# A reordered prologue in a ternary feed-forward kernel on one core: loads of W1, counting of masks, placing of gathered rows, PSUM banks

## The chip, the cores and the metric

The kernel runs on one core of a Trainium2 chip. The metric is the device time of one execution in microseconds (us); a lower one is better. Three runs of the kernel before gave a median of 972.73 us (972.67 to 972.78).

The core has four engines that compute. In the profile they are PE (TensorE: PE its matmuls, PEld the loading of their stationary operands), DVE (VectorE), ACT (ScalarE) and POOL (GpSimd). SP (SyncE) issues the transfers between HBM and the on-chip memory (SBUF), GpSimd the indirect gathers. TensorE writes its results to PSUM, eight banks of 512 f32 columns for 128 partitions. Every engine works through its own instructions in order and waits on semaphores for the others.

## The reference

```python
w = weights[conditions]                          # conditions (128,), weights (200, 64, 64)
c = jnp.einsum('bct,bcd->bdt', x, w)             # x (128, 64, 512)
def ternarize(W, threshold):                     # threshold 0.05
    absW = jnp.abs(W)
    delta = threshold * jnp.max(absW)
    mask = absW > delta
    n = jnp.maximum(jnp.sum(mask), 1)
    alpha = jnp.sum(jnp.where(mask, absW, 0.0)) / n
    return alpha * jnp.sign(W) * mask
h = gelu(c @ ternarize(W1).T + b1)               # W1 (2048, 512), exact gelu
y = h @ ternarize(W2).T + b2                     # W2 (512, 2048)
scale = jnp.max(jnp.abs(y)) / 7 + 1e-8
out = x + jnp.clip(jnp.round(y / scale), -7, 7) * scale
```

What matters here is ternarizing. No sign of W1 is known before the maximum of all of W1 is, since the threshold delta depends on it. The factor alpha, the sum of the magnitudes above delta divided by their number, is not needed for the first product: the kernel multiplies by the ternary signs and applies alpha where the gelu reads the product. So layer 1 can run ahead of alpha, as far as there are PSUM banks to keep its products in.

## The kernel before, in words

The batch of 128 goes in `NB` = 16 groups `n` of 8 batch elements, that is of four pairs (`PAIRS`), and 512 rows (`BLK`) of the layers' input. The hidden 2048 columns are 16 chunks `hc` (`NH`) of 128. The weights are held in four quarters `g` (`NG`) of four chunks. For accuracy every value is split into a high part (f32r) and a low part (f16), so every product is two rounds of matmuls, `k = 0` with a widened f32r copy of the ternary weights and `k = 1` with the narrow ones.

All instructions go through the helper `InOrder` (line 36): each engine gets them in the order of the program, and every line of the profile reads L36. So instructions are told apart by their tiles. The order is written out by hand.

The prologue, up to about 84 us, treats group 0 separately:

- Lines 113 to 140 issue the loads on SyncE: the conditions, W1 (tiles `nat`), in the pieces of `PIECES` (line 121: quarters 0 and 1 whole, quarter 2 in two, quarter 3 in three), x of group 0, b1, W2, b2. The transfers take eight semaphores in turn, so from the ninth on an issue waits until the transfer eight issues earlier has landed.
- Line 281: 50 matmuls on a tile of ones (`idle`), whose result nobody reads.
- Lines 284 to 297: VectorE takes the maximum of |W1| by pieces (tile `top`); ScalarE writes the signs and, in place, the magnitudes of quarters 0 to 2 (`sign1`, `abs1`); quarter 3's come later.
- `fetch` (line 174) gathers 128 rows of the conditioned weights for one pair by an indirect transfer from GpSimd into a tile of its own, `place` (line 186) copies them, times 64, as two 64x64 blocks into the diagonal tile `diag`, with GpSimd. Group 0's four pairs are fetched and placed ahead of the threshold, group 1's later in the prologue.
- `thresholds` (line 229): the maximum over the partitions with one TensorE transpose (`tops_delta_w`), then delta.
- `mix0` (line 303) multiplies x by `diag` into the four `py` banks; `hi0`, `lo0` split the result with ScalarE and VectorE.
- `mask1` and `signed1` (lines 325, 331) write masks and ternary signs of W1 (`masks`, `terns`) on VectorE; `widen1` (line 371) widens one chunk of `terns` on GpSimd into one of four buffers (`wf`).
- `early(hc)` (line 517) is layer 1 for chunk hc of group 0: 4 matmuls with `wf`, 4 with `terns`, into one of five banks in turn, two `ph` and the first three `py`. The fourth `py` bank holds `number`.
- `count1` (line 339) counts the masks: ones are stationary, the masks move through in pieces of 256 columns, 8 matmuls for each quarter. `above1` (line 350) sums the magnitudes above delta on ScalarE. `alpha_1` (line 535) makes alpha: VectorE reduces `number`, TensorE adds the sums over the partitions (`total`), VectorE finishes.
- `early_bend(hc)` (line 528) needs alpha: ScalarE reads the bank with the gelu (into a `ring` tile) and copies the high part `h`. The low part is a subtraction, by GpSimd for chunks 0, 2, 4 and 6, by VectorE for the others.

The order in which these were put is in lines 611 to 684: two chunks of layer 1, the count of quarter 0, chunk 2, the count of the other quarters, then `alpha_1`, whose second half (`next(find, None)`, the matmul `total`) stands inside chunk 3, ahead of its last two matmuls:

```python
    early(2)
    for g in range(1, NG):
        count1(g, number, False, g == NG - 1)
    find = alpha_1()
    next(find)
    early(3, lambda: next(find, None))
    widen1(0, 5)
    early(4)
    early_bend(0)
    widen1(0, 6)
```

From chunk 5 on a loop (lines 676 to 681) goes through `early(hc)`, `widen1(0, hc + 2)`, `early_bend(hc - 4)` and `behind(hc)`. `behind` spreads VectorE's work on W2 over the chunks: the maxima (`largest2`), the last ternary signs of W1, the threshold, whose transpose `ahead(11)` puts in front of chunk 11, and W2's signs (`signed2`). Behind it layer 2 of group 0 runs (lines 698 to 723) between the mixes of group 1 (`condition`), which take the two `ps_c` banks in turn. The groups behind follow in lines 963 to 1128.

## Time and profile before

| | |
|---|---|
| median of three runs | 972.73 us |
| the profiled execution | 972.58 us |
| its span, first to last instruction | 970.8 us |
| mean granted TensorE clock | 0.998 |
| TensorE busy / VectorE / ScalarE / GpSimd | 99% / 68% / 63% / 68% |
| TensorE's first block of layer 1 starts | 20.32 us |
| layer 2 of group 0 starts | 53.89 us |
| TensorE busy from 54 to 84 us | 30.00 of 30 us |

The page gives shares of the span and a chain of work that ended last, followed back from the last instruction. The timeline lists each engine's instructions in order of time: start, duration (of several, from the first's start to the last's end), engine, source line, operation, the tile written and the tiles read, the shape, and how many were merged; behind it, in brackets, how long the engine had been idle and what ended that. Matmul ends are modelled, and overlap the next matmul's start; so where TensorE waits, it is better seen from the starts.

### The profile page before, as it was taken

To read this page: it belongs to the slowest core of one execution; us is meant where nothing else is said; L and a number is where in the kernel's file an instruction comes from. 1 tells how busy PE (TensorE), PEld (TensorE's weight loads), DVE (VectorE), ACT (ScalarE), POOL (GpSimd) and SP (SyncE) were. 2 spreads that over 40 slices of the span, in tenths; PEclk is the share of its full clock that TensorE was granted. 3 is DMA by queue.
4 is the path that set the end of the run, shared out by engine and by line. 5 is a ranking of instruction groups with operands and counts; after the bars stand their busy time and mean duration, and the time that the engine had idled before them with its cause. 6 is when DMAs were issued, how large, how long until landed. Compare 5 with 4: busy or idle time off the path is not lost.

```text
span 970.8 us, 16879 instructions
## 1 busy us (share of the span) xinstructions
PE 960.1 (99%) x5858; PEld 727.4 (75%) x5858; DVE 659.7 (68%) x1143; ACT 613.7 (63%) x1076; POOL 662.0 (68%) x1024
## 2 busy tenths in 40 slices
PE   8999999999999999999999999999999999999996
PEld 5677667778788787887887787787887878766664
DVE  7898766666676666666666666666766765467856
ACT  7994445656656566665656666566666666467773
POOL 6877867777676676767677676776767776466541
PEclk9999999999999999999999999999999999999999
DMA  9201011010111100111110111101011111339994
GB/s 358 99 23 47 14 34 49 24 69 15 35 49 34 59 24 35 49 33 48 34 60 15 35 49 33 59 25 55 28 33 51 33 57 48 109 128 371 392 408 180
DMA packets 33158, 80.05 MB, mean 82 GB/s; under 512 B 3760, under 2 KB 3760, under 8 KB 30128
## 3 DMA queue, kind: packets, MB, share of 16 engines
q1 hardware_dynamic: 31024, 76.86, 22.0%
q0 software_dynamic: 2048, 2.10, 0.7%
q8 instruction: 47, 0.77, 0.3%
q14 instruction: 39, 0.32, 0.1%
HBM read 46.44 MB, written 32.51 MB: 81 GB/s over the span
## 4 chain that ended last, share of the span: by engine, by line
PE 97%; DVE 2%; ACT 0%; POOL 0%; issue 0%; ACTq 0%; POOLq 0%
PE py L36 46%; PE xy L36 18%; PE z L36 14%; PE ph L36 11%; PE pc L36 6%; PE idle L36 1%; DVE masks L36 1%; DVE xt L36 0%; DVE y_last L36 0%; DVE terns L36 0%; ACT diag L36 0%; PE number L36 0%; ACT ph L36 0%; DVE ymax L36 0%; DVE low_last L36 0%
## 5 line engine op out<-in xcount | busy, mean ns | idle before, releaser
L36 PE MATMUL py<-wf,h 128*128 128x512 f32 x1056 | 309.7, 418 | 0.0
L36 POOL CAST wf<-w2t 128x512 fp32r<-128x512 fp8e4 x236 | 205.6, 889 | 116.3 <-PE py L36 113.0
L36 DVE SCALAR_TENSOR_TENSOR low_parts<-ring,h 128x512 f16<-128x512 f32 x224 | 188.5, 877 | 85.9 <-ACT h L36 85.7
L36 PE MATMUL py<-w2t,low_parts 128*128 128x512 fp8e4 x944 | 228.0, 379 | 0.0
L36 PEld LDWEIGHTS py<-wf,h 128*128 128x128 f32 x1056 | 192.0, 189 | 44.8
L36 POOL CAST wf<-sums 128x256 fp32r<-128x256 fp8e4 (+1 forms) x288 | 142.1, 498 | 78.3 <-PE xy L36 75.2
L36 ACT ACTIVATE ring<-ring,b1t,alpha_up 128x512 f32<-128x512 f32 x192 | 155.9, 818 | 56.2 <-DVE ring L36 52.0
L36 DVE TENSOR_TENSOR ring<-xy,ring 128x256 f32<-128x256 f32 x192 | 106.6, 555 | 113.2 <-PE xy L36 113.2
L36 ACT COPY ring<-xy 128x256 f32<-128x256 f32 x192 | 71.6, 373 | 176.2 <-PE xy L36 175.0
L36 POOL CAST wf<-w1t 128x256 fp32r<-128x256 fp8e4 (+1 forms) x240 | 140.4, 596 | 27.8 <-PE ph L36 23.4
L36 PEld LDWEIGHTS <-low_parts 128*128 128x128 f16 x944 | 92.1, 98 | 88.8 <-issue 1.7
L36 ACT ACTIVATE h<-ring 128x512 fp32r<-128x512 f32 x224 | 130.3, 627 | 1.1
L36 POOL TENSOR_SCALAR diag<-wg 64x64 f32<-64x64 f32 x128 | 68.0, 532 | 40.0 <-DMA wg<-in_L_cond_weights,rows 36.1
L36 PEld LDWEIGHTS <-w1t 128*128 128x128 fp8e4 x768 | 63.4, 98 | 32.8 <-issue 12.8
L36 PE MATMUL xy<-xb,wf 128*128 128x256 f32 x384 | 84.7, 302 | 0.0
L36 PE MATMUL xy<-xt,wf 128*128 128x256 f32 x384 | 75.4, 277 | 0.0
L36 PE MATMUL xy<-xl,sums 128*128 128x256 f16 x384 | 75.3, 278 | 0.0
L36 POOL DMA_INDIRECT wg<-in_L_cond_weights,rows x64 | 63.0, 985 | 16.5 <-issue 13.7
L36 PE MATMUL xy<-xl,w1t 128*128 128x256 f16 x384 | 74.3, 275 | 0.0
L36 PE MATMUL ph<-x,wf 128*128 128x512 f32 (+1 forms) x260 | 73.2, 403 | 0.1
L36 PE MATMUL z<-xl,sums 128*128 128x256 f16 x384 | 73.2, 273 | 0.0
L36 ACT ACTIVATE ring<-ph,b1t,alpha_up 128x512 f32<-128x512 f32 x48 | 37.3, 777 | 54.7 <-PE ph L36 52.5
(133 smaller groups left out, 1421.8 us busy)
## 6 DMA issues: line engine op xcount, KB each, us to landing
xt<-in_x SPq DMA_DIRECT2D x38, 512.0 KB, 8.3
y_dram<-y SPq DMA_DIRECT2D x15, 1024.0 KB, 4.3
out<-xt SPq DMA_DIRECT2D x30, 512.0 KB, 8.2
x_quarters<-in_x SPq DMA_DIRECT2D x52, 256.0 KB, 2.7
nat<-in_L_ffn_W SPq DMA_DIRECT2D x6, 1024.0 KB, 10.2
y_back<-y_dram SPq DMA_DIRECT2D x2, 1024.0 KB, 10.7
nat<-in_L_ffn_W SPq DMA_DIRECT2D x3, 512.0 KB, 8.9
wg<-in_L_cond_weights,rows POOLq DMA_INDIRECT x64, 2.5
```

The source lines that it names most:

```text
L36: return lambda *args, **kw: self._tc.keep_in_program_order(make(*args, **kw))
```

## The change

The changed kernel differs in the prologue; in the groups behind, `fetch` and `place` only name their tiles in another way (these hunks are left out of the diff below).

- W1's quarters 0 to 2 are all loaded in two halves. Maxima and signs go by halves too; the magnitudes by quarters as before.
- 44 idle matmuls instead of 50.
- The four gathers of a group go into one tile; the pool holds one such tile instead of four of a pair each. In the prologue the rows are placed by `place_all`: two copies, one for each half of the partitions, instead of eight. Group 1's are placed in `behind(8)`, after the bend of chunk 4.
- `count1` makes the masks stationary, 128 columns at a time, and moves one column of ones through: 16 matmuls for each quarter, into one PSUM column, in a `ps_c` bank. Its sum over the partitions then needs one more matmul (`all1`), so alpha is made in three steps.
- Layer 1 of group 0 uses six banks, all four `py` and two `ph`; the first mixes take other banks for that.
- The order: `widen1(0, 0)` and `(0, 1)` go ahead of the gathers for group 1, `(0, 5)` ahead of the second two. Chunks 2 and 3 go ahead of the counts of quarters 0 and 1; the counts of quarters 2 and 3 stand inside chunk 4, `all1` and `total` inside chunk 5. W2's maxima begin in `behind(6)`, two at a time at first; the transpose for W2's threshold stands inside chunk 11; W2's sums go two, one, one instead of one, one, two.

```diff
@@ -73,7 +73,7 @@
 
     const = ctx.enter_context(tc.tile_pool(name="const", bufs=1))
     big = ctx.enter_context(tc.tile_pool(name="big", bufs=20))
-    gather = ctx.enter_context(tc.tile_pool(name="gather", bufs=PAIRS))
+    gather = ctx.enter_context(tc.tile_pool(name="gather", bufs=1))
     half = ctx.enter_context(tc.tile_pool(name="half", bufs=8))
     quarter = ctx.enter_context(tc.tile_pool(name="quarter", bufs=4))
     ps_c = ctx.enter_context(tc.tile_pool(name="ps_c", bufs=2, space=PSUM))
@@ -118,7 +118,7 @@
 
     nat1, nat2 = [], []
 
-    PIECES = [[slice(0, GH)], [slice(0, GH)], [slice(0, 2), slice(2, GH)]]
+    PIECES = [[slice(0, 2), slice(2, GH)]] * 3
     PIECES.append([slice(0, 2), slice(2, 3), slice(3, GH)])
     W1f = W1.rearrange("p k c h -> p k (c h)")
     for g in range(NG):
@@ -174,19 +174,26 @@
     def fetch(n, j):
 
         pair = n * PAIRS + j
-        wg = gather.tile([P, D], F32, tag="wg", name=f"wg_{pair}")
+        if j == 0:
+            gathered[n] = gather.tile([P, PAIRS, D], F32, tag="wg", name=f"wg_{n}")
         pool.indirect_dma_start(
-            out=wg[:, :],
+            out=gathered[n][:, j, :],
             out_offset=None,
             in_=table,
             in_offset=bass.IndirectOffsetOnAxis(ap=rows[:, pair : pair + 1], axis=0),
         )
-        return wg
-
-    def place(j, wg):
+
+    def place(n, j):
         for h in range(2):
             out = diag[half_of(h), j, h * D : (h + 1) * D]
-            pool.tensor_scalar(out, wg[half_of(h), :], UP, None, ALU.mult)
+            pool.tensor_scalar(out, gathered[n][half_of(h), j, :], UP, None, ALU.mult)
+
+    def place_all(n):
+        for h in range(2):
+            out = diag[half_of(h), :, h * D : (h + 1) * D]
+            pool.tensor_scalar(out, gathered[n][half_of(h)], UP, None, ALU.mult)
+
+    gathered = {}
 
     def parts(n):
         return [
@@ -262,24 +269,26 @@
     def group1(tiles, g):
         return tiles[g // 2][:, g % 2, :]
 
-    def sign1(g):
-        act.activation(group1(signs, g), flat(nat1[g]), AF.Sign)
+    def sign1(g, part=slice(0, WCH)):
+        act.activation(group1(signs, g)[:, part], flat(nat1[g])[:, part], AF.Sign)
+
+    parts1 = slice(0, WCH // 2), slice(WCH // 2, WCH)
+
+    mags = nat1[: NG - 1]
 
     def abs1(g):
 
         if g == NG - 1:
             mags.append(big.tile([P, GH, T], F32, tag="big", name="mag"))
-        else:
-            mags.append(nat1[g])
         act.activation(flat(mags[g]), flat(nat1[g]), AF.Abs)
-
-    mags = []
 
 
     idle = ps_h.tile([P, T], F32, tag="ph", name="idle")
     pool.memset(above[:, :T], 1.0)
-    for _ in range(50):
+    for _ in range(44):
         pe.matmul(out=idle, lhsT=ones_b, rhs=above[:, :T], start=True, stop=True)
+    for j in range(PAIRS):
+        fetch(0, j)
     at = 0
     for g in range(NG):
         for ks in PIECES[g]:
@@ -292,16 +301,16 @@
             )
             at += 1
         if g < NG - 1:
-            sign1(g)
+            for part in parts1:
+                sign1(g, part)
             abs1(g)
-    fetched = [fetch(0, j) for j in range(PAIRS)]
-    for j in range(PAIRS):
-        place(j, fetched[j])
+    place_all(0)
     two_next = parts(0)
     pcs = []
 
     def mix0(j):
-        pc = ps_y.tile([P, NT, P], F32, tag=f"py{j}", name=f"pc_0_{j}")
+        home, tag = [(ps_c, "pc"), (ps_h, "ph"), (ps_y, "py0"), (ps_y, "py1")][j]
+        pc = home.tile([P, NT, P], F32, tag=tag, name=f"pc_0_{j}")
         mix(pair_of(x_next, j), j, pc)
         pcs.append(pc)
 
@@ -336,15 +345,15 @@
             ALU.mult,
         )
 
-    def count1(g, number, first, final):
-        n = number.shape[1]
-        for i in range(WCH // n):
+    def count1(g):
+        for i in range(WCH // P):
             pe.matmul(
                 out=number,
-                lhsT=ones_b,
-                rhs=group1(masks, g)[:, i * n : (i + 1) * n],
-                start=(first and i == 0),
-                stop=(final and i == WCH // n - 1),
+                lhsT=group1(masks, g)[:, i * P : (i + 1) * P],
+                rhs=ones_b[:, :1],
+                start=(g == 0 and i == 0),
+                stop=(g == NG - 1 and i == WCH // P - 1),
+                skip_group_check=True,
             )
 
     def above1(g):
@@ -353,7 +362,6 @@
             above, flat(mags[g]), AF.Relu, bias=minus1, accum_out=sums1[:, g : g + 1]
         )
 
-    parts1 = slice(0, WCH // 2), slice(WCH // 2, WCH)
     wf1 = [half.tile([P, 2, NT, P], F32R, tag="half", name=f"wf1_{i}") for i in range(2)]
     w1f = [wf1[i // 2][:, i % 2] for i in range(4)]
     cond = {0: two_next}
@@ -413,14 +421,13 @@
                     stop=(c == NT - 1 and k == 1),
                 )
 
-    def layer1_0(n, hc, ph, part=slice(0, BLK), between=None):
+    def layer1_0(n, hc, ph, part=slice(0, BLK), between={}):
         g, i = divmod(hc, GH)
         narrow = group1(terns, g)[:, i * T : (i + 1) * T].rearrange("p (c h) -> p c h", c=NT)
         for k in range(2):
             w = narrow if k else wide1[n, hc]
             for c in range(NT):
-                if between is not None and k == 1 and c == NT - 2:
-                    between()
+                between.get((k, c), lambda: None)()
                 pe.matmul(
                     out=ph,
                     lhsT=w[:, c, :],
@@ -514,9 +521,9 @@
     ring = [t[:, i, :] for t in rings for i in range(2)]
     ring += [quarter.tile([P, BLK], F32, tag="quarter", name=f"ring_{i}") for i in (10, 11)]
 
-    def early(hc, between=None):
-
-        slot = (hc + 1) % 5
+    def early(hc, between={}):
+
+        slot = (hc + 4) % 6
         if slot < 2:
             ph = ps_h.tile([P, BLK], F32, tag="ph", name=f"ph_0_{hc}")
         else:
@@ -535,8 +542,11 @@
     def alpha_1():
 
         count = const.tile([P, 1], F32, name="count1")
-        dve.tensor_reduce(count, number, AX.X, ALU.add)
-        dve.tensor_scalar(count, count, 1.0, None, ALU.max)
+        dve.tensor_copy(count, number)
+        yield
+        all_of = ps_c.tile([P, 1], F32, tag="pc", name="all1")
+        pe.matmul(out=all_of, lhsT=ones_f, rhs=count, start=True, stop=True)
+        dve.tensor_scalar(count, all_of, 1.0, None, ALU.max)
         dve.reciprocal(count, count)
         yield
         total = ps_c.tile([P, NG], F32, tag="pc", name="total1")
@@ -610,10 +620,10 @@
 
     mask1(0, parts1[0])
     signed1(0, parts1[0])
-    fetched += [fetch(1, j) for j in range(2)]
     widen1(0, 0)
     widen1(0, 1)
-    fetched += [fetch(1, j) for j in range(2, PAIRS)]
+    for j in range(2):
+        fetch(1, j)
     lo0(0)
     lo0(1)
     hi0(2)
@@ -629,41 +639,43 @@
     abs1(3)
     for g in range(NG):
         above1(g)
-    number = ps_y.tile([P, T // 2], F32, tag="py3", name="number")
-    count1(0, number, True, False)
+    early(2)
+    number = ps_c.tile([P, 1], F32, tag="pc", name="number")
+    count1(0)
     mask1(1)
     signed1(1)
     widen1(0, 4)
-    for j in range(PAIRS):
-        place(j, fetched[PAIRS + j])
+    early(3)
+    count1(1)
     mask1(2)
     mask1(3)
     signed1(2)
-    early(2)
-    for g in range(1, NG):
-        count1(g, number, False, g == NG - 1)
+    widen1(0, 5)
+    for j in range(2, PAIRS):
+        fetch(1, j)
+    widen1(0, 6)
+    early(4, {(1, 0): lambda: count1(2), (1, 2): lambda: count1(3)})
     find = alpha_1()
     next(find)
-    early(3, lambda: next(find, None))
-    widen1(0, 5)
-    early(4)
+    early(5, {(0, 2): lambda: next(find), (1, 2): lambda: next(find, None)})
+    widen1(0, 7)
     early_bend(0)
-    widen1(0, 6)
+    early_bend(1)
     wf2 = half.tile([P, 2, T], F32R, tag="half", name="wf2")
     w2f = [wf2[:, i, :] for i in range(2)]
     w2f += [quarter.tile([P, T], F32R, tag="quarter", name=f"wf2_{i}") for i in (2, 3)]
     find = thresholds("w2", top_2, above.bitcast(F32)[:, :P])
 
 
-    def ahead(hc):
-        if hc == 11:
-            next(find)
-
     def behind(hc):
-        if 5 <= hc < 5 + NG:
+        if hc == 6:
+            largest2(0)
+        if 6 <= hc < 6 + NG - 1:
             largest2(hc - 5)
         if hc == 7:
             sign1(3)
+        if hc == 8:
+            place_all(1)
         if hc == 9:
             signed1(3)
         if hc == 11:
@@ -676,9 +688,8 @@
         if hc in (13, 14):
             widen2(0, hc - 13)
 
-    for hc in range(5, NH):
-        ahead(hc)
-        early(hc)
+    for hc in range(6, NH):
+        early(hc, {(1, 2): lambda: next(find)} if hc == 11 else {})
         if hc + 2 < NH:
             widen1(0, hc + 2)
         early_bend(hc - 4)
@@ -718,10 +729,10 @@
         if hc in (5, 7, 9, 11):
             j = (hc - 5) // 2
             condition(1, j, pair_of(x_next, j), two_next)
-            for g in {7: [0], 9: [1], 11: [2, 3]}.get(hc, []):
+            for g in {7: [0, 1], 9: [2], 11: [3]}.get(hc, []):
                 sum2(g)
     cond[1] = two_next
-    x_next, two_next, fetched = [], [], []
+    x_next, two_next = [], []
     hf = ring[:2]
     widen1(1, 0)
     widen2(0, NH - LAG)
...
```

More of the change, by code (lines that the diff above doesn't have):

```diff
@@ L987, in eight @@
             if 2 <= hc < 2 + PAIRS:
-                fetched.append(fetch(n + 1, hc - 2))
+                fetch(n + 1, hc - 2)
             if 7 <= hc < 7 + PAIRS:
-                place(hc - 7, fetched[hc - 7 - PAIRS])
+                place(n + 1, hc - 7)
         if n == KNOWN and hc in (0, 1):
@@ L1089, in behind @@
                 if k < PAIRS:
-                    fetched.append(fetch(n + 1, k))
+                    fetch(n + 1, k)
                 if 2 <= k < 2 + PAIRS:
-                    place(k - 2, fetched[PAIRS * (n - 1) + k - 2])
+                    place(n + 1, k - 2)
                 if not leaves:
```

## Prediction

> **What bounds the kernel now.** I read the page's share of busy time, then the chain that ended last, then the first 90 us engine by engine in the timeline.
>
> ```profile
> PE 960.1 (99%) x5858; PEld 727.4 (75%) x5858; DVE 659.7 (68%) x1143; ACT 613.7 (63%) x1076; POOL 662.0 (68%) x1024
> ...
> PE 97%; DVE 2%; ACT 0%; POOL 0%; issue 0%; ACTq 0%; POOLq 0%
> ```
>
> TensorE is the bound, and from 31.6 us on the chain runs through it alone until the tail. So a change in the prologue is worth what it moves TensorE's position at the end of the prologue, no more: a later start of everything behind is passed on to the end one for one. I call `early(k)` block k. This is TensorE, out of its timeline:
>
> ```profile
> 2.96 13.62 PE L36 MATMUL idle<-junk,ones_b 128*128 128x512 bf16 x50 [2.96 <-POOL junk L36]
> 16.42 0.27 PE L36 MATMUL tops_delta_w<-ident_f,first 128*128 128x128 f32 x1
> ...
> 20.32 0.74 PE L36 MATMUL ph<-x,wf 128*128 128x256 f32 x4
> ...
> 24.07 1.04 PE L36 MATMUL number<-masks,ones_b 128*128 128x256 bf16 x8
> ...
> 26.80 1.91 PE L36 MATMUL number<-masks,ones_b 128*128 128x256 bf16 x16
> 29.07 1.03 PE L36 MATMUL number<-masks,ones_b 128*128 128x256 bf16 x8 [0.36 <-DVE masks L36]
> ...
> 31.32 0.28 PE L36 MATMUL total<-sums,ones_f 128*128 128x4 f32 x2
> ...
> 35.79 1.20 PE L36 MATMUL ph<-x,wf 128*128 128x512 f32 x4
> ```
>
> Block 0 starts at 20.32, the counting takes 0.82 us at 24.07 and 3.06 us (0.5 of it waiting) at 26.80, the total of the sums goes out at T = 31.32 after three and three quarter blocks, and block 6 starts at 35.79. Of the other engines these lines matter:
>
> ```profile
> 32.38 0.78 ACT L36 ACTIVATE ring<-ph,b1t,alpha_up 128x512 f32<-128x512 f32 x1 [1.31 <-PE ph L36]
> ...
> 37.70 1.91 ACT L36 ACTIVATE signs<-nat 128x2048 bf16<-128x2048 f32 x1
> ...
> 40.31 0.62 ACT L36 CAST h<-ring 128x512 fp32r<-128x512 f32 x1
> ```
> ```profile
> 41.01 2.32 POOL L36 TENSOR_TENSOR h<-ring,h 128x512 fp32r<-128x512 f32 x1 [1.79 <-ACT h L36]
> 43.28 1.16 POOL L36 CAST wf<-terns 128x512 fp32r<-128x512 bf16 x2
> ```
> ```profile
> 32.21 8.86 DVE L36 TENSOR_REDUCE top<-nat 128x1 f32<-128x2048 f32 x4
> 40.98 1.21 DVE L36 TENSOR_TENSOR terns<-masks,signs 128x2048 bf16<-128x2048 bf16 x1
> ```
>
> T starts everything on these three. The first gelu runs at T+1.06. ScalarE is then full: four bends, the last sign, bend 4, whose copy ends at T+9.6. GpSimd's subtraction for block 4 waits for that copy (its 1.79 us idle) and runs at T+9.69. Behind it in GpSimd's order stands the widening for block 11, ready at 43.89 where TensorE wanted it near 44.9: one microsecond to spare. VectorE's maxima of W2 also start at T+0.9.
>
> **Part by part.** *Start of block 0.* W1's last quarter keeps its three pieces. Its first piece lands at 12.90 (SyncE's next issue on that lane), the last at 14.41. VectorE now reaches it without backlog: 12.93 + 1.13 + two of 0.6, the last after 14.41, ends near 15.3, not 15.48. So the halves bring 0.15 us. Six idle matmuls of 0.216 us less free TensorE at 15.1, and the transpose goes at 15.9, not 16.42. Of x the halves land at 15.8 and 17.1 (issue plus 10.9 and 11.0 us), just in time; x is issued two lanes later but its queue holds W1 until 14.4, so I cost that at nothing (up to 0.5 us if the queue ran dry). The gathers land at 14.08; eight copies ended at 17.05, two end near 15.4. Signs in halves cost ScalarE three times some 0.17 us, but it starts them on the first half and ends 1 us earlier. Together block 0 starts at 19.8: gain 0.5.
>
> *The wait for block 2.* It now follows block 1 directly, at 19.8 + 1.84 + 1.91 = 23.5 (blocks at 20.32, 22.16, 24.07). Its widening needs VectorE's second half of terns, at 22.55 now (23.17 less 0.6), and runs beside VectorE's masks, where three casts took 4.66 us at 23.28, so 1.56 and not 0.6: ready at 24.2. Wait 0.7 (none if the cast ran at 0.6).
>
> *Counting.* 32 matmuls of 256 columns become 64 with one column, each with its own weights. The trace has no such matmul. From above, the 109 ns from start to start of the 256 columns; from below, 11 ns: where a bf16 weight load has nothing to hide it (behind block 1's f32 half) the next matmul comes after 227 instead of 216 ns. The two 4-column matmuls of the total start 29 ns apart. I take 29 + 11 = 40 ns, nearest to these rows: 2.6 us (0.7 to 7.0).
>
> The Trainium skill, "TensorE: Matmul & The Clock Gate", section "LDWEIGHTS (loading the stationary operand)", gives columns / 1.2 ns, 107 ns for 128, which would make 6.8 us and speaks against the change; its section on Fast Weight Load speeds up loads that are not FP32. The f32 rows agree with 107 (333 against 229 ns), the bf16 rows do not (11 ns), so the measurement decides; by the first rule the sum below would be 4.2 us more.
>
> *T.* In the new order the total stands at three quarters of block 5, not of block 3. Blocks 0 to 4 take 1.84, 1.91, 1.91 and twice 1.85, three quarters of 5 with the new column sum 1.6: 11.0 us. T = 19.8 + 11.0 + 0.7 + 2.6 = 34.1, against 31.32: **2.8 us later**, with ScalarE's sums long ready (31.06 less 0.6). That is not itself lost, as TensorE worked; what waits for T is.
>
> *Six banks.* Block 6 takes block 0's bank, which the first gelu gives back at T+1.84 plus 0.06. TensorE is done with block 5 at T+0.57. **Wait 1.3**: block 6 at 36.0, against 35.79. Five banks asked that of block 5, but a whole block lay between.
>
> *Placing the rows of group 1* (eight copies at 27.91 to 33.0 before, hidden, as block 6's widening was ready at 35.74 and TensorE there at 35.64) now stands behind the subtraction for block 4 and ahead of the widening for block 11. Both chains hang on T as before, so the subtraction again meets VectorE's signs and takes 2.27 to the next start. One 64x256 copy: from below a 64x64 one, 0.37, from above four, 1.46; 0.65 as a 512-wide cast at 0.6 is nearest. Widening ready at T + 9.69 + 2.27 + 1.3 + 0.61 + 0.05 = T+13.9 = 48.0. TensorE would be there at T + 1.9 + 1.92 + 4 x 1.805 = T+11.0. **Wait 2.9.** Block 11 with the transpose now inside ends at 48.0 + 2.0 = 50.0, against 46.67: 3.3 us late.
>
> *W2's threshold.* The transpose goes at block 11's three quarters, 49.5 against 44.94, so VectorE's full row of signs and low parts up to 74 us runs 4.55 us late, TensorE 3.3. The third mix of group 1 (74.08) needs a bank whose last reader ends at 73.50: slack 0.55, so 0.65 more (0 to 1.2, by how VectorE's passes fall beside GpSimd). Two W2 sums ahead of the third low part end near 88, TensorE needs it near 88.4: nothing. Later steps keep their order on GpSimd, gathers included, with the same waits: the one gather tile is refilled four steps after its last copy. Nothing.
>
> Sum: 3.3 + 0.65 = **4.0 us** on the profiled execution's 972.58 us (span 970.8), 976.6; the runs' median is 972.73, 0.15 from it, within what I can resolve. About 0.2%, 1.95 us, is what a measurement of this kernel can tell from no change.
>
> **Rivals.** *Forecast, 0.66:* 974.5 to 978.5, by counting at 20 to 60 ns (1.3 us either way) and row copies of 0.45 to 1.0 us. *Dear counting, 0.08:* if the 109 ns hold for one column too, T moves by 64 x 69 ns more: 4.4 us, 981.0. For it speaks that no matmul of the trace repeats faster for long, against it the 11 and 29 ns. *Nothing much, 0.16:* counting at 15 ns (1.6 us less), the cast of block 2 at 0.6 (0.7 less), the late bank of the third mix without effect (0.65 less): 4.0 - 2.95 = 1.05, so 973.6. It also covers that the edits reach less than they say, as the halves of W1 do.
>
> *Not slower, 0.10:* the counting is nearly free and TensorE's lead survives. At 11 ns T falls to 32.2 and block 6 to 34.1, 1.7 us ahead of 35.79. The lead is worth 1.7 us at the end, 970.9, if the widening for block 11 is ready when TensorE comes, at T+11.0; from there on each microsecond that it is late costs one. For it: GpSimd sat idle 1.79 us ahead of the subtraction, time enough for the two copies. Against it: in the changed order the copies stand behind the subtraction, and the subtraction waits for ScalarE, not for GpSimd.
>
> The range takes in the forecast and most of the two cases at its sides: 973.9 to 979.4. Of the chances, faster by over 0.2% is a part of the last case, 0.06; within 0.2% the rest of it and most of "nothing much" (up to 974.7), 0.16; slower 0.78.
>
> **What would show it.** The total near 34.1 (31.32); TensorE idle about 1.3 us ahead of block 6 and 2.9 ahead of block 11, the latter put down to GpSimd's casts; 64 `number` matmuls in some 2.6 us; the transpose for W2 near 49.5. Wrong if block 11 starts before 45.5, or if the counting takes over 4 us.

## The result, and the profile after

The changed kernel took 977.5 us (median of 6 runs, 976.93 to 979.17); the kernel before took 972.68 us beside it (6 runs, 972.49 to 972.78). The ratio is 1.0054, with a 95% interval of 1.0041 to 1.0067: slower by half a per cent. The forecast was 976.6 us, with a range of 973.9 to 979.4. The profiled execution took 977.55 us, with a span of 975.7 us and a mean granted clock of 0.997.

The page of the changed kernel, share of busy time and chain of work that ended last:

```profile
PE 958.8 (98%) x5886; PEld 726.3 (74%) x5886; DVE 658.7 (68%) x1145; ACT 614.1 (63%) x1079; POOL 653.4 (67%) x1012
...
PE 94%; DVE 1%; issue 1%; POOL 1%; DMA 1%; ACT 0%; SPq 0%; POOLq 0%; ACTq 0%
```

TensorE is busy 1.3 us less and the span is 4.9 us longer, so TensorE stands idle some 6 us more. GpSimd has come into the chain with 1%. Where that is, TensorE's timeline shows (start, duration, and in brackets the idle time ahead and what ended it):

```profile
16.29 0.33 PE L36 MATMUL tops_delta_w<-ident_f,first 128*128 128x128 f32 x1 [1.57 <-DVE first L36]
...
19.95 0.72 PE L36 MATMUL ph<-x,wf 128*128 128x256 f32 x4
...
24.65 1.19 PE L36 MATMUL ph<-x,wf 128*128 128x512 f32 x4 [0.66 <-POOL wf L36]
...
26.55 0.54 PE L36 MATMUL number<-ones_b,masks 128*128 128x1 bf16 x16
26.96 1.19 PE L36 MATMUL ph<-x,wf 128*128 128x512 f32 x4
...
33.56 0.28 PE L36 MATMUL total<-sums,ones_f 128*128 128x4 f32 x2
...
35.54 1.17 PE L36 MATMUL ph<-x,wf 128*128 128x512 f32 x4 [1.25 <-ACT ring L36]
...
48.03 1.96 PE L36 MATMUL ph<-x,wf 128*128 128x512 f32 x4 [3.22 <-POOL wf L36]
...
50.66 0.42 PE L36 MATMUL tops_delta_w<-ident_f,junk 128*128 128x128 f32 x1
...
51.37 1.39 PE L36 MATMUL ph<-x,wf 128*128 128x512 f32 x4
```

In the kernel before, the transpose for W2 stands just ahead of block 11, and block 12 follows:

```profile
44.94 0.27 PE L36 MATMUL tops_delta_w<-ident_f,junk 128*128 128x128 f32 x1
...
46.67 1.28 PE L36 MATMUL ph<-x,wf 128*128 128x512 f32 x4
```

Read the starts. Block 0 is at 19.95 (20.32 before), the total at 33.56 (31.32), block 6, after a wait for ScalarE to give back block 0's bank, at 35.54 (35.79). So up to here TensorE is ahead of the kernel before, by 0.25 us. Then it waits 3.22 us for block 11's widened weights, and block 12 starts at 51.37, against 46.67: 4.70 us late. The second `total`, in the groups' first part, is at 93.38 instead of 88.56 (4.82), and the span is 4.9 longer. So nearly everything was lost ahead of block 12.

Of the 4.70 the wait is only 3.22. The other part stands in the durations: block 11 took 3.34 us from start to start, where it took 1.73 before, each with the transpose. The windows of 4 us show why (busy time and instructions of PE, PEld, DVE, ACT and POOL, then the granted clock, DMA share and GB/s):

```profile
44.00:48.00 4.00, 0.81 (x4) 0.20 (x2) 1.53 (x3) 3.91 (x7) 3.85 (x5) 1.00 0.62 183
48.00:52.00 4.00, 3.97 (x11) 2.38 (x12) 0.78 (x4) 3.21 (x6) 3.45 (x5) 0.57 0.21 81
```

In the window behind the wait the granted clock is 0.57 in the mean. In windows of 0.1 us it is 1.00 until 48.1 and 0.50 from 48.2 to 51.6: TensorE, idle for 3.2 us, came back at its full clock, fell to half of it within 0.2 us and ran so for 3.4 us.

What it waited for, on GpSimd:

```profile
43.25 2.31 POOL L36 TENSOR_TENSOR h<-ring,h 128x512 fp32r<-128x512 f32 x1 [2.06 <-ACT h L36]
45.53 1.77 POOL L36 TENSOR_SCALAR diag<-wg 64x256 f32<-64x256 f32 x2
47.37 1.16 POOL L36 CAST wf<-terns 128x512 fp32r<-128x512 bf16 x2
```

GpSimd idles 2.06 us for ScalarE's copy `h` of block 4, subtracts, then places group 1's rows (1.77 us for two copies), and only then widens for block 11, which starts 0.05 us after the first of the two casts has ended. The copies need nothing that was not there 2 us earlier; they stand at that place because the order was written so.

### The profile page after: what moved, and what is told of

It is laid out like the page before. It is cut to its first block, busy times and chain, and to the rows that moved or that the text cites. A ratio compares the mean times of both kernels' runs of the same rounds, so it can differ in the third digit from the quotient of the medians.

```text
span 975.7 us, 16928 instructions
## 1 busy us (share of the span) xinstructions
PE 958.8 (98%) x5886; PEld 726.3 (74%) x5886; DVE 658.7 (68%) x1145; ACT 614.1 (63%) x1079; POOL 653.4 (67%) x1012
## 4 chain that ended last, share of the span: by engine, by line
PE 94%; DVE 1%; issue 1%; POOL 1%; DMA 1%; ACT 0%; SPq 0%; POOLq 0%; ACTq 0%
PE py L36 46%; PE xy L36 18%; PE z L36 13%; PE ph L36 10%; PE pc L36 6%; DMA nat<-in_L_ffn_W 1%; POOL wf L36 1%; DVE xt L36 0%; SPq L36 0%; POOL wg L36 0%; DVE y_last L36 0%; DVE top L36 0%; ACT diag L36 0%; POOL diag L36 0%; ACT ph L36 0%
## 5 line engine op out<-in xcount | busy, mean ns | idle before, releaser
L36 POOL CAST wf<-w1t 128x256 fp32r<-128x256 fp8e4 (+1 forms) x240 | 140.3, 595 | 28.0 <-PE ph L36 23.5
L36 POOL TENSOR_SCALAR diag<-wg 64x64 f32<-64x64 f32 (+1 forms) x116 | 65.5, 565 | 41.1 <-DMA wg<-in_L_cond_weights,rows 37.9
```

Source lines behind the costliest of these rows:

```text
L36: return lambda *args, **kw: self._tc.keep_in_program_order(make(*args, **kw))
```

## The experiments

The theory after the result: the 4.9 us are the late widening for block 11 (the row copies in front of it, and T, the total, 2.24 us later) and the clock that falls behind the wait. Rivals: that the copies' place is innocent; that the clock's fall is no part of it; that the later T costs by another way. All times below are medians, with the lowest and highest run; each ratio is to the kernel before, run beside it. What is called `e6` and so on is the name of a run.

**e1: place first.** The changed kernel with the row copies taken out of `behind(8)` and put ahead of `early_bend(4)`, so ahead of the subtraction, in GpSimd's idle time.

```diff
-        if hc == 8:
-            place_all(1)
...
             widen1(0, hc + 2)
+        if hc == 8:
+            place_all(1)
         early_bend(hc - 4)
```

> Changed kernel, with group 1's two row copies put ahead of the subtraction for block 4 on GpSimd instead of behind it; all else the same. Queue theory (block 11 waits because the copies, 1.83 us, stand between the subtraction and its widening, and the clock drops because that gap is over 3 us): the copies fit into GpSimd's 2.06 us of idle time ahead of the subtraction, block 11 starts near 46.15 instead of 48.03 with a gap of 1.5 us, at full clock, so 1.9 + 1.65 us less: near 974.0 us. Rival (the late total is the whole cause, the copies are innocent): block 11 still waits about 3 us and the time stays near 977.5.

Measured: 974.37 us (974.16 to 976.04), 1.0021 (1.0012 to 1.0030). TensorE's timeline:

```profile
45.75 1.21 PE L36 MATMUL ph<-x,wf 128*128 128x512 f32 x4 [1.36 <-POOL wf L36]
```

The wait is 1.36 instead of 3.22, and block 11 takes 1.85 us at full clock. 3.1 of the 4.9 us went by moving two instructions.

**e2: the wait filled.** The changed kernel with 52 matmuls of ones by ones ahead of block 11, whose result nobody reads; all else as it was.

```diff
+        if hc == 11:
+            filler = ps_c.tile([P, P], F32, tag="pc", name="filler")
+            for _ in range(52):
+                pe.matmul(out=filler, lhsT=ones_b, rhs=ones_b, start=True, stop=True)
         early(hc, {(1, 2): lambda: next(find)} if hc == 11 else {})
```

> Changed kernel, with 52 matmuls of 128 columns on ones, result unread, put into TensorE's gap ahead of block 11 (some 2.9 us of work in a gap of 3.2). The wait for GpSimd stays. Clock theory (the idle gap halves the granted clock for the 3.3 us behind it): block 11 still starts near 48.03 but runs at full clock, 8 matmuls in 1.95 us with the transpose and not 3.34, so 1.4 us less: near 976.1, with a smaller spread of the runs. Rival (block 11 is slow for another reason, its operands or GpSimd's traffic): still 3.3 us for block 11 and about 977.5.

Measured: 976.12 us (976.08 to 976.29), 1.0036 (1.0022 to 1.0050).

```profile
44.50 3.07 PE L36 MATMUL filler<-ones_b 128*128 128x128 bf16 x52
47.90 1.20 PE L36 MATMUL ph<-x,wf 128*128 128x512 f32 x4 [0.33 <-POOL wf L36]
```

Block 11 starts where it did (47.90, against 48.03), with useless work ahead of it instead of a pause, and 1.4 us are gone. So that part of the loss is the clock's and not the wait's. The five runs lie within 0.2 us, the six of the changed kernel over 2.2 us. A part of that spread may come from this place too, but not all: e1 and e3, where block 11 runs at full clock, also have runs 1.2 us and more above their medians (one of 11, two of nine).

**e9: before, with the copies late.** The other direction: the kernel before, with only its eight row copies of group 1 moved into `behind(8)`, behind the subtraction for block 4.

```diff
-    for j in range(PAIRS):
-        place(j, fetched[PAIRS + j])
     mask1(2)
...
+        if hc == 8:
+            for j in range(PAIRS):
+                place(j, fetched[PAIRS + j])
```

> Kernel before the change, with only the eight row copies of group 1 moved behind the subtraction for block 4 on GpSimd, where the change has its two. Queue theory: the total stays near 31.3, but block 11 (44.96) waits for its widening behind eight copies of 0.42 us and more, until 47.4 if VectorE leaves GpSimd alone and until 49 or so if W2's signs, from 46 on, hold it: 974.9 to 978, the middle 976.5. Rival (the place of the copies is innocent, the late total did it): 972.6.

Measured: 980.60 us (979.44 to 981.26), 1.0080 (1.0066 to 1.0094); more than the theory's range. TensorE, then GpSimd, then two windows:

```profile
50.16 2.07 PE L36 MATMUL ph<-x,wf 128*128 128x512 f32 x4 [5.00 <-POOL wf L36]
```
```profile
43.24 4.23 POOL L36 TENSOR_SCALAR diag<-wg 64x64 f32<-64x64 f32 x8
47.54 3.58 POOL L36 CAST wf<-terns 128x512 fp32r<-128x512 bf16 x2
```
```profile
48.00:52.00 4.00, 1.84 (x4) 1.16 (x4) 4.00 (x4) 0.82 (x2) 4.00 (x3) 0.57 0.00 0
52.00:56.00 4.00, 4.00 (x12) 2.12 (x12) 3.96 (x2) 1.40 (x2) 4.00 (x3) 0.58 0.00 0
```

The total stands at 31.26, unmoved, and still the kernel loses 8 us. So the place of the copies is enough by itself, and the rival falls. The size was off twice: the eight copies took 4.23 us and the casts behind them 1.8 each, so the wait is 5.00 us; and the clock stayed near 0.57 for two windows.

**e3: the widening for block 11 moved too.** e1, and the widening for block 11 ahead of the subtraction as well.

```diff
-        if hc + 2 < NH:
+        if hc + 2 < NH and hc != 9:
             widen1(0, hc + 2)
+        if hc == 8:
+            place_all(1)
+            widen1(0, 11)
...
```

> Changed kernel, with group 1's row copies and also the widening for block 11 ahead of the subtraction for block 4 on GpSimd. Queue theory: no gap ahead of block 11 (44.64), the widening for block 12 is ready near 46.5 where TensorE comes near 46.6; of the waits only the one for block 0's bank (1.25 us) stays. Block 12 starts near 46.6 as before the change (46.67), so near 972.6 us. Rival (the late total is the whole cause): about 977.5, or one of the later blocks takes the wait over.

Measured: 974.32 us (973.75 to 976.11), 1.0021 (1.0011 to 1.0031): a miss by 1.7 us. Block 11 no longer waits, but later ones do, and GpSimd shows why:

```profile
48.95 1.21 PE L36 MATMUL ph<-x,wf 128*128 128x512 f32 x4 [0.71 <-POOL wf L36]
...
51.58 1.21 PE L36 MATMUL ph<-x,wf 128*128 128x512 f32 x4 [0.53 <-POOL wf L36]
```
```profile
47.29 13.48 POOL L36 CAST wf<-terns 128x512 fp32r<-128x512 bf16 x9
```

GpSimd has no idle time from 40.9 to 60.8, and its nine casts take 13.48 us, 1.5 each instead of 0.6: from here VectorE works on W2's signs beside them. What GpSimd owes is only handed on to blocks 13 and 14. That the late T starts this chain is argued here, not shown; it leads to e4.

**e4: the total earlier.** The changed kernel with the counts of quarters 2 and 3 ahead of block 4, and the sums over partitions inside block 4.

```diff
-    early(4, {(1, 0): lambda: count1(2), (1, 2): lambda: count1(3)})
+    count1(2)
+    count1(3)
     find = alpha_1()
     next(find)
-    early(5, {(0, 2): lambda: next(find), (1, 2): lambda: next(find, None)})
+    early(4, {(0, 3): lambda: next(find), (1, 2): lambda: next(find, None)})
+    early(5)
```

> Changed kernel, with the counts of quarters 2 and 3 ahead of block 4 and the sum of the count and the total inside block 4 instead of block 5. The total goes near 31.75 instead of 33.56. Queue theory: the wait for block 0's bank goes (1.25 us), block 6 starts near 34.1, but the copies still stand ahead of the widening for block 11, ready near 46.2: the gap ahead of block 11 stays at 3.0 us, block 11 is 1.85 us earlier than in the changed kernel, 975.6 us with the clock drop and 974.2 without. Rival (the late total is the whole cause): all of the loss goes, 972 or less.

Measured: 976.20 us (975.31 to 979.81), 1.0037 (1.0025 to 1.0049). The total comes 11.8 us after block 0 instead of 13.6, and the wait for block 0's bank is gone. Block 11 still waits 2.93 us, and that pause, shorter than the changed kernel's, also brought the clock to 0.50, from 50.8 to 54.3 us in windows of 0.1 us. Behind block 0 the trace has block 6 1.61 us earlier than the changed kernel and block 13 1.79, and the three lowest runs (975.31 to 975.56) meet the 975.6 expected. So the later T costs some 1.8 us, most of it ahead of block 6. The other three runs lie higher, and the profiled one, the highest, showed something new, at the threshold:

```profile
17.48 0.47 PE L36 MATMUL tops_delta_w<-ident_f,first 128*128 128x128 f32 x1 [3.14 <-DVE first L36]
17.74 6.50 PE L36 MATMUL pc<-diag,xt 128*128 128x128 f32 x32
...
50.27 1.61 PE L36 MATMUL ph<-x,wf 128*128 128x512 f32 x4 [2.93 <-POOL wf L36]
```

W1's last piece landed at 15.90 here (14.33 to 14.84 in the 13 other traces), TensorE stood 3.14 us after its 44 idle matmuls, and the first 32 matmuls of the mixes took 6.50 us instead of 3.75, with a granted clock of 0.50 from 16.7 to 23.5 us. The other two high runs of e4 (976.84 and 978.21) are put down to the same, but have no profile.

**e6: both, and one widening.** e4, the row copies ahead of the first `early_bend(0)`, and the widening for block 11 ahead of `early_bend(4)`.

```diff
     widen1(0, 7)
+    place_all(1)
     early_bend(0)
...
-        if hc + 2 < NH:
+        if hc + 2 < NH and hc != 9:
             widen1(0, hc + 2)
+        if hc == 8:
+            widen1(0, 11)
...
-        if hc == 8:
-            place_all(1)
```

> Changed kernel, with three moves on hand-written places and nothing taken out: the counts of quarters 2 and 3 ahead of block 4 with the total inside block 4; group 1's two row copies ahead of the subtraction for block 0 on GpSimd (2.56 us of idle time there); the widening for block 11 ahead of the subtraction for block 4. Theory (the loss is the queue behind late alpha, not the edits themselves): total near 31.7, no wait for block 0's bank, block 11 and block 12 without a gap, block 15 ends near 52.3 where before the change it ended at 53.9; some 0.6 us come back at the third mix of group 1, so near 971.3, below the kernel before. Rival (one-column counts, six banks or the single gather tile cost by themselves): not below 973.

Measured: 973.90 us (971.91 to 974.71), 1.0008 (0.9999 to 1.0017). The median says little here: five runs lie at 971.91 to 972.40 with a mean granted clock of 0.997 to 0.999, six at 973.90 to 974.71 with 0.996. The lower ones are near the 971.3 expected. The profile, one of them, shows no wait for GpSimd behind block 2 in the prologue, but 1.77 us of idle time ahead of the threshold, and 0.75 ahead of the third mix of group 1, for VectorE.

**e7: W1 whole again.** e6, with quarters 0 and 1 of W1 loaded and signed whole, as before.

```diff
-    PIECES = [[slice(0, 2), slice(2, GH)]] * 3
+    PIECES = [[slice(0, GH)], [slice(0, GH)], [slice(0, 2), slice(2, GH)]]
...
-            for part in parts1:
-                sign1(g, part)
+            sign1(g)
```

> The same as the run with the three moves, but W1's first two quarters loaded whole and signed whole, as before the change (the maximum of quarters 0 and 1 in one pass each). Theory (the last landing of W1, not the pieces, sets the threshold): within 0.3 us of the run with the three moves, 971.3 to 971.6. Rival (the halves pay, a microsecond at VectorE): 972.3. Rival (the halves make W1 land later): 970.9.

Measured: 972.73 us (972.27 to 973.93), 1.0001 (0.9992 to 1.0010): only one of 11 runs in the upper cluster, but the others some 0.4 us higher than e6's lower cluster. Where these 0.4 us come from is not settled. VectorE ended the maxima at 15.41 in this trace and at 15.54 in e6's; over the traces it did so at 15.41 to 15.53 with whole quarters (five) and at 15.32 to 15.54 with halves (seven, without the late landings of the changed kernel's trace, 15.77, and e4's, 16.95), so they show no gain of the halves beyond 0.1 us. Why the upper cluster is nearly gone is not shown either. The idle time ahead of the threshold was 0.95 us in this profile against 1.77 in e6's, but 0.55 of that is that the 44 idle matmuls ended later, at 15.01 against 14.46.

**e8: 50 idle matmuls.** e6 with 50 idle matmuls ahead of the threshold, as the kernel before has them.

```diff
-    for _ in range(44):
+    for _ in range(50):
```

> The same as the run with the three moves, but with 50 idle matmuls instead of 44. Theory (between the last idle matmul and the threshold TensorE waits; where W1 lands late that gap passes 2 to 3 us and the clock halves for the mixes): the transpose goes 0.4 us later, so 971.7 in the middle, but without the runs that lie 2 us and more above the others. Rival (the high runs of the changed kernel come from elsewhere): the same spread as with 44.

Measured: 972.28 us (971.90 to 972.61, 11 runs), 0.9995 (0.9986 to 1.0004). The upper cluster is gone, and the edit touches little but the idle time ahead of the threshold: the six matmuls that the change took away had covered it. That the clock fell there in the upper runs is read from e4's trace and from their mean clock (0.996); none of them was profiled. Behind block 2 one wait remains, ahead of the third mix:

```profile
73.88 1.16 PE L36 MATMUL pc<-diag,xt 128*128 128x128 f32 x8 [1.13 <-DVE x L36]
```

**e10: a third bank for the mixes.** The kernel that the expectation means is e8.

```diff
-    def condition(n, j, xp, two):
-        pc = ps_c.tile([P, NT, P], F32, tag="pc", name=f"pc_{n}_{j}")
+    def condition(n, j, xp, two, space=ps_c, tag="pc"):
+        pc = space.tile([P, NT, P], F32, tag=tag, name=f"pc_{n}_{j}")
...
-            condition(1, j, pair_of(x_next, j), two_next)
+            condition(1, j, pair_of(x_next, j), two_next, *([(ps_h, "ph")] if j == 2 else [(ps_c, "pc")])[0])
```

> The kernel of the run before last but one (row copies and one widening moved ahead of block 0 and block 4, the count's chain taken into block 4, 50 idle matmuls) with one edit: the third mix of group 1 writes to one of the banks of the blocks instead of the two banks of the mixes. In that kernel's trace TensorE stood 1.1 us ahead of the third mix, put down to VectorE's addition of an earlier mix. Theory: the wait is for the bank and all of it is on the path, so it goes and nothing takes its place: 972.28 - 1.1 = 971.2 us (971.0 to 971.5). Rival: VectorE is late there anyway, and the time comes back ahead of the tiles of group 1 behind it: 972.3 us.

Measured: 971.79 us (971.54 to 972.21, 11 runs), 0.9992 (0.9983 to 1.0001): between the two. The wait at the mix is gone, and most of it comes back ten microseconds later, on VectorE's mixed rows:

```profile
83.44 1.02 PE L36 MATMUL ph<-x,w1t 128*128 128x512 f16 x4 [0.86 <-DVE x L36]
```

**e11: a count in the wait for block 2.** e10, with the count of quarter 0 ahead of block 2.

```diff
-    early(2)
     number = ps_c.tile([P, 1], F32, tag="pc", name="number")
     count1(0)
+    early(2)
```

> The kernel of e10 with the one-column count of the first quarter put ahead of block 2 instead of behind it. TensorE waits 0.66 us ahead of block 2 for GpSimd's widening in the changed kernel, and 16 such matmuls took 0.41 us there. Theory: the count moves into the wait and 0.4 us go: 0.4 us below e10, about 970.8 us. Rival: the masks of the first quarter are not ready when block 1 ends, so the count waits itself and block 2 is as late as before: the same as e10.

Measured: 971.10 us (970.89 to 972.25, 11 runs), 0.9987 (0.9978 to 0.9996), beside 972.59 of the kernel before.

```profile
23.59 0.54 PE L36 MATMUL number<-ones_b,masks 128*128 128x1 bf16 x16
24.40 1.19 PE L36 MATMUL ph<-x,wf 128*128 128x512 f32 x4 [0.27 <-POOL wf L36]
```

The wait for block 2 fell from 0.65 to 0.27, as the theory has it; that is 0.4 of the 0.7 us. The other 0.3 is not settled: in this trace the wait for VectorE's mixed rows is 0.26 us instead of e10's 0.86, and the transpose at the threshold went 0.45 us earlier, and one trace does not tell which of this is the edit's. This version is the fastest: 1.5 us below before, with the interval just clear of 1, and 6.4 below the changed kernel (the latter across two sets of runs).

**e12: the counting alone.** The kernel before with only the one-column counting.

```diff
-        for i in range(WCH // n):
+        for i in range(WCH // P):
             pe.matmul(
                 out=number,
-                lhsT=ones_b,
-                rhs=group1(masks, g)[:, i * n : (i + 1) * n],
+                lhsT=group1(masks, g)[:, i * P : (i + 1) * P],
+                rhs=ones_b[:, :1],
...
```

The hunks left out add the sum over the partitions (`all1`) inside chunk 3 and make `number` one column wide.

> The kernel before with only the counting of the change: 64 matmuls with one column each instead of 16 with 512, and the sum over the partitions by one more matmul, all in the order of before otherwise. The changed kernel's trace gave 25 ns from start to start, 1.6 us for 64, where before's 16 took 3.4 us. Theory: before's masks of the last quarter end at 29.03 us and hold the count there, and the added sum over partitions costs a part of what is left: total 0.3 to 0.4 us earlier than 31.32, 972.3 us (971.9 to 972.6). Rival: the whole 1.8 us come off: 970.9 us. Rival: the count's extra trip through VectorE costs more than it brings: 973 us or more.

The kernel before counts with 32 matmuls of 256 columns, not with 16 of 512 as the expectation says.

Measured: 973.64 us (972.43 to 975.35, 11 runs), 1.0009 (1.0000 to 1.0018). TensorE, and a window:

```profile
26.62 0.54 PE L36 MATMUL number<-ones_b,masks 128*128 128x1 bf16 x16
27.52 0.55 PE L36 MATMUL number<-ones_b,masks 128*128 128x1 bf16 x16 [0.36 <-DVE masks L36]
29.07 0.55 PE L36 MATMUL number<-ones_b,masks 128*128 128x1 bf16 x16 [1.00 <-DVE masks L36]
29.48 1.05 PE L36 MATMUL ph<-x,wf 128*128 128x512 f32 x3
```
```profile
28.00:32.00 4.00, 3.00 (x27) 2.00 (x25) 2.57 (x5) 2.72 (x4) 3.68 (x6) 0.77 0.02 7
```

The counting is 1.7 us cheaper, and the last of it starts at 29.07 exactly as before: VectorE's masks hold it. And then the clock falls, without any long wait, to 0.50 from 30.2 to 33.6 us in windows of 0.1 us.

**e13: the counting alone, pauses filled.** e12 with 5 and 15 matmuls of ones where it waited.

```diff
+        if g > 1:
+            filler = ps_c.tile([P, P], F32, tag="pc", name=f"filler_{g}")
+            for _ in range(5 if g == 2 else 15):
+                pe.matmul(out=filler, lhsT=ones_b, rhs=ones_b, start=True, stop=True)
         count1(g, number, False, g == NG - 1)
```

> The kernel of e12 (before with only the one-column counting), plus matmuls of ones by ones whose result nobody reads: 5 ahead of the count of quarter 2 and 15 ahead of that of quarter 3, in places where TensorE waited 0.36 and 1.00 us for masks in e12's trace (57 ns each in an earlier run, so 0.29 and 0.86 us). In e12 the granted clock fell to 0.77 and 0.80 between 28 and 36 us; from 26.62 to 29.48 TensorE had there done nothing but 48 matmuls with one column each and waits of 1.36 us together. Theory: so little work counts as a pause for the clock, and the drop costs the 1.1 us between e12's median, 973.64, and its three lowest runs (972.43 to 972.77): with the pauses filled the clock stays full and the median is 972.4 us (972.2 to 972.6). Rival: the clock falls for another reason, and the time stays at 973.6 us.

Measured: 972.57 us (972.41 to 972.75, 11 runs), 0.9999 (0.9990 to 1.0008).

```profile
28.00:32.00 4.00, 3.86 (x47) 2.89 (x45) 2.92 (x7) 2.71 (x4) 3.69 (x6) 1.00 0.02 7
```

The clock stays, and the upper runs are gone. (e13 ran on another chip than e12; the kernel before took 972.68 and 972.59 us beside them.) What is left is the counting by itself, and it is worth nothing in that order: the total at 31.31, against 31.32 before. The count's end is set by the masks, and block 3, with the added sum over the partitions inside, takes 0.37 us longer up to the total, about as much as the last count saves (0.41 us instead of 0.79).

## Why the prediction was right, and where it was not

The direction, the place and the mechanism held. The prediction said that the wait ahead of block 11 would be GpSimd's, with the row copies between the subtraction and the widening; the trace shows it so, and e1 and e9 show it from both sides.

- *Start of block 0*: 19.95, forecast 19.8. The 0.15 us that the halves should bring is not seen in this trace: W1's last piece landed at 14.84 (14.41 before), the first piece of its last quarter reached VectorE at 13.37 instead of 12.93, and the maxima ended at 15.77 instead of 15.3. The landing differs from run to run by more than the 0.15, and the other traces show 0.1 us at most for the halves (e7). TensorE, with six idle matmuls less, stood 1.57 us. Costing these six at a plain gain was too simple: e8 shows that they are a cover, which saves about 2 us in six of the 11 runs of e6.
- *The wait for block 2*: 0.66, forecast 0.7.
- *Counting*: mis-sized. 16 matmuls took 0.41 us from start to start, 26 ns each and 1.6 us for 64; the forecast took 40 ns and 2.6. The two rows it leaned on, 29 ns and 11 ns, should not have been added. The 107 ns that the Trainium skill gives in "TensorE: Matmul & The Clock Gate", section "LDWEIGHTS (loading the stationary operand)", are four times too dear for these bf16 masks. The same page has a floor of about 25 ns from start to start for small matmuls, in its section "Wait — 56ns, not 53.3ns?"; the measured 26 ns agree with that one, weight load included.
- *T*: 33.56, forecast 34.1, early mostly by the counting.
- *Six banks*: the wait ahead of block 6 was 1.25, forecast 1.3. e4 takes it away by the order alone.
- *The row copies*: mis-sized, 1.84 us for two up to the next instruction's start (45.53 to 47.37), not 1.3. With T early by 0.54 and the copies dearer by 0.54 the two errors cancel, and block 11 starts at 48.03 where the forecast had 48.0. That it met is luck; the wait, 3.22 against 2.9, shows an error.
- *The step that failed*: "Block 11 with the transpose now inside ends at 48.0 + 2.0 = 50.0". It ended at 51.37. Block 11 ran at a granted clock of 0.50 for nearly all its time and took 3.34 us; with the pause filled it took 1.83 (e2). So the term left out is 1.3 us against the forecast's 2.0, and 1.5 against e2. The prediction had found the 2.9 us pause and still priced what follows it at full clock. In e4 a pause of just that length, 2.93 us, had the clock at 0.50 for 3.4 us behind it. The same page of the Trainium skill says in its section "What's actually happening" that TensorE falls to half its clock after an idle window of about 3.4 us, and that the window runs free of the kernel. The runs agree on the half; as to the pause, less was enough here (2.93).
- *Third mix of group 1*: 0.65 forecast, none seen. The transpose for W2 came at 50.66, 5.72 us later than before, and VectorE's step behind it 5.88 later (51.12 against 45.24). But its chain from there up to the mixed rows ran 0.86 us shorter, so they were 5.02 late (77.84 against 72.82) and TensorE 4.81; the slack of 0.55 covers that. Why the chain was shorter is not shown; single passes in it took other times, beside other work of GpSimd. The same wait is real where TensorE is earlier: 0.75 in e6, 1.13 in e8.

So at block 12 the forecast had 3.3 us and the trace has 4.7: block 11 starts where the forecast had it and takes 3.34 us instead of 2.0. At the end the sum of 4.0 stands against a measured 4.8. It is nearer than its parts, as the 0.65 of the third mix, which did not come, makes up for half of the 1.3 that was left out; that is luck too.

The case "Not slower" was near in its first step: with the counting at 26 ns TensorE had a lead at block 6, though 0.25 us and not the 1.7 it had at 11 ns. It had the copies fit into GpSimd's idle time ahead of the subtraction for block 4, and said against itself that the order does not put them there; that decided. Where they do stand there, in e1, the kernel is still 1.8 us slower than before. e11, which moves the total, the copies and more, is 1.5 us faster; that this is near the 1.7 of that case proves nothing for it.

What stays open: why W1's last piece lands up to 1.5 us later in some executions, and why the 44 idle matmuls end anywhere from 14.33 to 15.01 us in the traces; what the halves of W1 do to the upper runs (e7); the 0.3 us of e11 beyond the wait; and whether one-column matmuls count as a pause for the clock or only the waits among them do. e13 filled the waits, and did not change the matmuls.

## What to carry to other kernels

Where an engine works through a written order, an instruction that needs nothing new should not stand behind one that waits: two copies moved by one place were 3.1 us here. A pause of TensorE that comes near 3 us is to be priced with the slow stretch that can follow it, here 1.3 to 1.5 us more, and matmuls that do nothing are worth keeping where the pause cannot be helped. Work made cheaper on the bounding engine (the counting, 1.7 us) is worth something only if what it waits for, here the masks, is not what ends it.

## What the runs showed of the hardware

- In windows of 0.1 us the granted clock fell to 0.50 at pauses of 2.93 and 3.14 us (e4), 3.22 us (the changed kernel) and 5.00 us (e9). At pauses of 1.36 us (e1) and 1.77 us (e6's profile) it stayed at 1.00. In the prologue no trace has a pause between 1.77 and 2.93 us.
- At these four pauses it fell 2.4 to 3.5 us after the last matmul had ended. In the changed kernel TensorE had been back at work for 0.2 us by then, at e4's block 11 for 0.6.
- The same pause near 3 us does not always end in a slow start. Every trace has one of 2.93 to 2.98 us in its tail, ahead of the matmul `tops_top_rest`; in six of the 14 this matmul took 0.47 to 0.48 us, with the clock at 0.50, in the other eight 0.33, with the clock at 1.00.
- The stretch at 0.50 lasted 3.4 us in the changed kernel, at e4's block 11 and in e12, and twice that, 6.8 us, in e9 and at e4's threshold.
- The clock also fell, to 0.77 over a window of 4 us, where TensorE did 48 one-column matmuls with waits of 0.36 and 1.00 us among them for 2.86 us (e12), and not when the waits were filled (e13).
- One-column matmuls with new bf16 weights each follow each other at 26 ns.
- At the same place of GpSimd's order two copies of 64x256 f32 took 1.77 us (the changed kernel) and eight of 64x64, with the same data, 4.23 us (e9, where VectorE was busy for 2.66 us of the window from 44 to 48, and for 1.53 in the changed kernel). A cast of 128x512 took 0.6 us where VectorE stood idle (the changed kernel, at 47.37) and 1.5 to 1.8 us beside VectorE's passes (e3, e9).
